# One layout [w, sample] for all activations, and group statistics by TensorE, in a four-layer residual net

## The chip, the cores and the metric

The kernel runs on one core of one Trainium2 chip. The metric is the time on the device in microseconds, the median of several runs. The core has five engines that run side by side and wait for each other through semaphores: TensorE (PE in the profile; its weight loads are shown as PEld), VectorE (DVE), ScalarE (ACT), GpSimd (POOL) and SyncE (SP), which here only issues DMAs. TensorE reads SBUF and writes PSUM[...].

## The reference

The input x has 8192 samples of 8 channels, 16 rows (h) and 16 columns (w). Four layers follow each other, and each adds the result of a layer to the unnormalized x. `_gn` normalizes over 4 groups of 2 channels.

```python
x = x + tt_matvec([core0, core1, core2], _gn(x)) + bias                # layer 0: three small factors, rank 8
x = x + relu(batchnorm(conv3x3(_gn(x), lin_w) + lin_b.sum(0)))         # layer 1: statistics over all samples
# layer 2: both sides quantized to 127 steps, one scale over all of _gn(x)
x = x + conv3x3(quantize(_gn(x)), quantize(weight)) / (sx * sw) + bias
# layer 3: weights are signs times a mean, padding repeats the edge
x = x + conv3x3(pad_edge(_gn(x)), sign(weight) * mean|weight|) + bias
```

## The kernel before, in words

**Tiles.** 128 samples make a tile, so there are 64 tiles of 128 partitions x 2048 floats. A partition is a pair (channel, row); along the free axis lie the 128 samples and the 16 columns w. Convolutions over rows and channels are matmuls with a banded 128 x 128 matrix, and the three taps over w are three matmuls whose moving operand is shifted by one column. Before, the free axis of x and all that comes of it is [sample, w]: the 16 columns of a sample lie side by side. The input is brought into that order on the host, as "xt"; a second copy, "xb", has another order that layer 0 contracts first.

**Stage 1 (lines 319 to 677)** does layer 0 and the convolution of layer 1. The loop runs over 256 quarter tiles n of 32 samples. `expand` contracts w into u (rank 8 x w) for the next quarter, in two groups k of 8 matmuls; each group fills the PSUM tile pu, of which there is one (`ps_u`, bufs=1), and `act.copy` moves it to u (2048 elements a partition). `main` multiplies u by core01 in eight accumulating matmuls r = 0 to 7 into po; a fp32 matmul shows as two instructions. The order is written out: `at(r, ...)` puts a step ahead of the r-th matmul of `main`. The first group of `expand` stands at r = 0, the second at r = 4. `norm_sums` and `norm_b_square` issue a square on ScalarE at r = 1 in two of four quarters, `limbs` a cast at r = 2; `conv1_scaled` follows at r = 6 and the two evacuations of `conv1` at the end. po, pm and pc share three PSUM slots (`ps_m`), so each po needs that the former po has been added to x by VectorE. `norm_sums` and `norm_stats` reduce x and its square over w (`reduce_w`), in the quarter q = 0 of the next tile. `conv1_output` writes y with w in steps of four.[...]

**Stage 2 (lines 745 to 857)** reads x and y from DRAM, applies batch norm and relu, adds, and takes the statistics of layer 2: `sums_pe` (8 matmuls of 512 columns into four strips of 32 PSUM partitions), a reduction over w and a transpose on VectorE (`stats2`), a power on GpSimd, and `to_rows` (a masked copy and a transpose on VectorE) with two matmuls in `spread2`. `centre2` subtracts the mean, `range2` takes the largest magnitude. Most tiles go back to DRAM; 13 stay in SBUF.

**Stage 3 (lines 879 to 1053)** does layers 2 and 3. For each tile: `scale2` (v, int8), `round2` (q, bf16), `layer2` (12 matmuls pq), `first2` on VectorE for one half and `second2` and `add2` on ScalarE and GpSimd for the other, the statistics of layer 3 (`square3`, `sums3`, `stats3`, `pow3`, `rows3`, `spread3`), `scale3` (t), `high3` and `low3` (t split in two fp32r parts, rows of 16 columns with an edge on each side, 18 in all), `layer3` (24 matmuls pf), `add3` and `finish`. The order of the steps of different tiles is C_HEAD, then TURN repeated, then C_TAIL (lines 48 to 69 and 1040 to 1047).

The access to u and the copy that fills it, and the one that fills core01 at the start:

```python
pu = ps_u.tile([P, 4, 2, 2 * R * W], F32, name=f"pu_{t}_{q}_{k}", tag="pu")
act.copy(T[t]["u", q][:, 16 * k:16 * k + 16].rearrange("p b n -> p (b n)"), pu.rearrange("p i j n -> p (i j n)"))
c01v = core01.rearrange("p s (n h) -> p n h s", n=C)
act.copy(c01v[:, n:n + C // 2], cps[:, n:n + C // 2].rearrange("p n (h s) -> p n h s", s=R))
```

Of the kernel before, what the change touches and what calls it, by code (L numbers as in the profile page):

```python
# [47 lines left out]
C_HEAD = """  # L48
rows2:0 spread2:0 v:0 rows2:1 q:0 spread2:1 c2h1:0 rows2:2 bias:0 v:1 spread2:2 rows2:3 c2h0:0 v:2 z1:0 q:1
spread2:3 stz:0 add1:0 bias:1 c2h1:1 sq:0 c2h0:1 z1:1 v:3 sums:0 stz:1 small:0 q:2 add1:1 c2h0:2 c2h1:2 bias:2  # L50
rows2:4 pow:0 sq:1 rows2:5 rows3:0 z1:2 spread2:4 spread3:0 stz:2 t:0 q:3 sums:1 hi:0 c:0 small:1 v:4 add1:2 pow:1
bias:3 c2h0:3 spread2:5 rows3:1 sq:2 c2h1:3 spread3:1 stz:3 lo:0 sums:2 t:1 rows2:6 corr:0 edl:0 small:2 c:1 q:4
z1:3 hi:1 c3h0:0 pow:2 c3h1:0 v:5 add1:3 rows3:2 out0:0 bias:4 out1:0 lo:1 sq:3 q:5 spread3:2 spread2:6 c2h0:4 c:2
corr:1 edl:1 c2h1:4 rows2:7 z1:4 stz:4 t:2 hi:2 sums:3 c3h1:1 small:3 v:6 c3h0:1 out1:1 c2h1:5 pow:3 bias:5 rows3:3
spread3:3 lo:2 out0:1 q:6 spread2:7 rows2:8 z1:5 edl:2 v:7 c:3 add1:4 sq:4 c2h0:5 c3h0:2 bias:6 t:3 corr:2 stz:5
sums:4 c3h1:2 small:4 add1:5 hi:3 out0:2 c2h0:6 pow:4 rows3:4 sq:5 out1:2 spread2:8 stz:6 spread3:4 t:4 lo:3 c2h1:6
z1:6 corr:3 edl:3 sums:5 c:4 hi:4 small:5 pow:5 bias:7 v:8 q:7 add1:6
""".split()
C_TAIL = """
c2h1:-4 sq:-5 rows2:-2 rows3:-6 out1:-8 spread3:-6 rows2:-1 spread2:-2 c2h0:-4 v:-2 sums:-5 stz:-4 z1:-4 q:-3 t:-6  # L60
edl:-7 c3h0:-7 q:-2 small:-5 c2h1:-3 c:-6 out0:-7 c2h0:-2 hi:-6 add1:-4 sq:-4 pow:-5 rows3:-5 z1:-3 spread3:-5
bias:-2 t:-5 stz:-2 lo:-6 edl:-6 sums:-4 small:-4 bias:-3 corr:-6 c:-5 spread2:-1 c2h0:-3 stz:-3 pow:-4 c3h1:-7
hi:-5 out1:-7 c3h0:-6 rows3:-4 spread3:-4 add1:-3 c2h1:-2 sq:-3 lo:-5 z1:-2 out0:-6 v:-1 c3h1:-6 edl:-5 q:-1 add1:-2
sums:-3 t:-4 corr:-5 c:-4 c3h1:-5 out1:-6 small:-3 sq:-2 pow:-3 hi:-4 out1:-5 lo:-4 rows3:-3 bias:-1 sums:-2 c2h1:-1
small:-2 z1:-1 spread3:-3 edl:-4 c2h0:-1 c3h0:-5 c:-3 t:-3 stz:-1 add1:-1 pow:-2 corr:-3 rows3:-2 c3h1:-4 hi:-3
spread3:-2 sq:-1 out0:-5 c:-2 corr:-4 sums:-1 t:-2 lo:-3 hi:-2 small:-1 pow:-1 out1:-4 c3h0:-4 corr:-2 rows3:-1
out0:-4 edl:-3 c3h0:-3 spread3:-1 t:-1 lo:-2 c3h1:-3 out0:-3 edl:-2 out1:-3 hi:-1 c:-1 lo:-1 c3h0:-2 c3h1:-2 edl:-1
out0:-2 c3h0:-1 out1:-2 corr:-1 c3h1:-1 out0:-1 out1:-1
""".split()

# [8 lines left out]
def tile_net(ctx: ExitStack, tc: tile.TileContext, xb, xt_in, pack0, pack1, pack2, out):  # L79
# [84 lines left out]
    def late_constants(late):  # L164
# [99 lines left out]
        mod32 = const.tile([P, 32], F32, name="mod32")  # L264
# [5 lines left out]
        for k, name in enumerate(("sel0", "sel1", "corr")):  # L270

            t = L[name] = const.tile([P, CH], F32, name=name)
            dve.tensor_copy(t.rearrange("p (g n) -> p g n", g=G),
                            mod32[:, G * k:G * k + G].unsqueeze(2).to_broadcast([P, G, CH // G]))
        yield "statistics"

    def diagonal(n):
        ts = []
        for k in range(2):
            t = const.tile([P, NQ, 32], F32, name=f"diag_{n}_{k}")  # L280
            nc.gpsimd.memset(t, 0.0)
            ts.append(t)
        return ts
# [6 lines left out]
    HALVES = [(0, P // 2), (P // 2, P)]  # L290

    def samples(t):
        return t.rearrange("p (b w) -> p b w", w=W)

    def over_w(stat, a, b):

        return stat[:, a:b].unsqueeze(2).to_broadcast([P, b - a, W])

    def reduce_w(dst, src, op=ALU.add):
        for a, b in HALVES:  # L300
            dve.tensor_reduce(dst[:, a:b], samples(src)[:, a:b], AX.X, op)
# [21 lines left out]
    with first as s:  # L323
# [13 lines left out]
        x1n = [const1.tile([P, P, W + 2], F32, name=f"x1n_{k}") for k in range(2)]  # L337
        for t in x1n:
            pool.memset(t[:, :, 0:W + 2:W + 1], 0.0)
# [13 lines left out]
        def add_bias(t):  # L353
            v = samples(T[t]["x"])
            pool.tensor_tensor(v, v, bias0_t.unsqueeze(1).to_broadcast([P, P, W]), ALU.add)
# [56 lines left out]
        def expand(t, q, k):  # L412

            if k == 0:
                T[t]["u", q] = us[q % 2].rearrange("p (b n) -> p b n", b=QS)
# [8 lines left out]
            else:  # L424
                xv = T[t]["xl", q].rearrange("p (i n m) -> p i n m", i=4, m=CH)
                for i in range(4):
                    for j in range(2):
                        pe.matmul(pu[:, i, j], xv[:, i, 2 * k + j], L["core2r"], start=True, stop=True)
            act.copy(T[t]["u", q][:, 16 * k:16 * k + 16].rearrange("p b n -> p (b n)"),
                           pu.rearrange("p i j n -> p (i j n)"))  # L430

        def main(t, q, between, n0=None):
            u = T[t].pop(("u", q)).rearrange("p b (s n) -> p b s n", s=R)
            po = ps_m.tile([P, BANK], F32, name=f"po_{t}_{q}", tag="mm")
            parts = [(0, QS)] if n0 is None else [(0, n0), (n0, QS)]
            for a, b in parts:
                for r in range(R):
                    for f, args in between.get(r, ()) if b == QS else ():
                        f(*args)
                    pe.matmul(samples(po)[:, a:b], core01[:, r], u[:, a:b, r, :], start=(r == 0), stop=(r == R - 1))  # L440
            cols = slice(q * BANK, (q + 1) * BANK)
            x = T[t]["x"]
            dve.tensor_tensor(x[:, cols], po, x[:, cols], ALU.add)
# [12 lines left out]
        def norm_apply(t):  # L456
            group_spread(spread1, T[t].pop("mv"), 32)
            x, xn = samples(T[t]["x"]), x1n[t % 2][:, :, 1:W + 1]
            for a, b in HALVES:
                for k, op, i in ((0, ALU.subtract, x), (1, ALU.mult, xn)):  # L460
                    dve.tensor_tensor(xn[:, a:b], i[:, a:b], over_w(spread1[:, k], a, b), op)


        def quarter_stats(t, q):
            cols, x = slice(q * BANK, (q + 1) * BANK), T[t]["x"]
            sums = small.tile([P, 2, QS], F32, name=f"sq_{t}_{q}", tag="sums")
            act.activation(xh[:, cols], x[:, cols], AF.Square)
            for k, src in enumerate((x, xh)):
                dve.tensor_reduce(sums[:, k], samples(src)[:, q * QS:(q + 1) * QS], AX.X, ALU.add)
# [3 lines left out]
        def quarter_apply(t, q):  # L473
            spread = spreads[q % 2]
            group_spread(spread, T[t].pop(("mv", q)), 32)
            b = slice(q * QS, (q + 1) * QS)
            x, xn = samples(T[t]["x"])[:, b], x1n[t % 2][:, b, 1:W + 1]
            for k, op, i in ((0, ALU.subtract, x), (1, ALU.mult, xn)):
                dve.tensor_tensor(xn, i, over_w(spread[:, k], 0, QS), op)
# [4 lines left out]
        def conv1_scaled(t, q):  # L484

            x = x1n[t % 2][:, q * QS:(q + 1) * QS]
            x4, x2 = (wk.tile([P, QS, n], F32, name=f"{k}_{t}_{q}", tag=k, bufs=1) for k, n in (("x4", W), ("x2", W // 2)))
            act.activation(x4, x[:, :, 0:W], AF.Copy, scale=4.0)
            act.activation(x2, x[:, :, 1:W:2], AF.Copy, scale=2.0)
            T[t]["x4", q] = x4, x2  # L490

        def conv1_input(t, q):
            x = x1n[t % 2][:, q * QS:(q + 1) * QS]
            x4, x2 = T[t].pop(("x4", q))
            e, r = (wk.tile([P, n, QS, W // 4], F32, name=f"{k}_{t}_{q}", tag=k, bufs=1) for k, n in (("e", 4), ("r", 2)))
            v = wk.tile([P, 6, QS, W // 4], F32, name=f"v_{t}_{q}", tag="v")
            pool.tensor_tensor(e.rearrange("p k b j -> p b j k"), *(t.rearrange("p b (j k) -> p b j k", k=4)
                                                                    for t in (x[:, :, 2:W + 2], x4)), ALU.subtract)
            pool.tensor_tensor(r[:, 0], x2[:, :, 1:W // 2:2], x2[:, :, 0:W // 2:2], ALU.subtract)
            pool.tensor_tensor(r[:, 1], x[:, :, 4:W + 1:4], x[:, :, 2:W:4], ALU.subtract)  # L500
            pool.tensor_tensor(v[:, 0], e[:, 2], e[:, 1], ALU.add)
            pool.tensor_tensor(v[:, 1], e[:, 2], e[:, 1], ALU.subtract)
            pool.tensor_tensor(v[:, 2], r[:, 1], r[:, 0], ALU.add)
            pool.tensor_tensor(v[:, 3], r[:, 1], r[:, 0], ALU.subtract)
            pool.tensor_tensor(v[:, 4:6], e[:, 2:4], e[:, 0:2], ALU.subtract)
            T[t]["v", q] = v.rearrange("p i b j -> p i (b j)")
# [14 lines left out]
        def conv1_direct(t, q):  # L521

            x = x1n[t % 2][:, q * QS:(q + 1) * QS]
            po = ps_m.tile([P, BANK], F32, name=f"pd_{t}_{q}", tag="mm")
            for k in range(3):
                pe.matmul(samples(po), L["band1"][:, k], x[:, :, k:k + W], start=(k == 0), stop=(k == 2))
            act.activation(T[t]["y"][:, q * BANK:(q + 1) * BANK], po, AF.Identity, bias=L["b1"], scale=1.0)
# [5 lines left out]
        def conv1_stats(t, q):  # L533
            dve.bn_stats(T[t]["bst"][:, q], T[t]["y"][:, q * BANK:(q + 1) * BANK])
# [6 lines left out]
        def conv1_output(t, q):  # L541
# [7 lines left out]
            s1, d3, d1, s3 = sd[:, 0], sd[:, 1], pm[:, 1], pm[:, 3]  # L549
            y = T[t]["y"][:, q * BANK:(q + 1) * BANK].rearrange("p (n k) -> p k n", k=4)  # L550
            ends = wk.tile([P, 2, NC], F32, name=f"ends_{t}_{q}", tag="ends", bufs=1)
            dve.tensor_tensor(ends[:, 0], s1, po[:, 0], ALU.add)
            dve.scalar_tensor_tensor(ends[:, 1], d3, 8.0, po[:, 1], ALU.mult, ALU.add)
# [154 lines left out]
    def sums_pe(ps, x, sq):  # L708

        for k, src in ((0, x), (1, sq)):  # L710
            for q in range(NQ):
                pe.matmul(ps[32 * q:32 * q + 32], L["wsum"][:, k], src[:, q * BANK:(q + 1) * BANK],
                          start=(k == 0), stop=(k == 1))


    def put_quarter(ps):
# [406 lines left out]
```

## Time and profile before

| | |
|---|---|
| median of 3 runs | 3833.41 us (3831.76 to 3834.64) |
| span of the profiled execution | 3831.5 us |
| PE, DVE, POOL, ACT busy | 94%, 89%, 79%, 66% |
| moved by DMA | 960.93 MB, mean 251 GB/s |

A row of the profile names engine, operation, output<-input by the program's names, the shapes, the count, then the busy time in all, the mean ns of one, and the idle time of the engine before it with what ended it. Busy time counts overlapping instructions once, so the mean of a matmul, which holds its latency, is longer than the distance from one to the next. The profiled execution is one run; its span is compared with what is worked out from its rows.

### The profile page before, as it was taken

The numbers are of one execution on the slowest core, as the hardware profiler recorded it, in microseconds if no ns is written. First come the engines' busy times: TensorE is split into PE (matmuls) and PEld (weight loads), VectorE is DVE, ScalarE is ACT, GpSimd is POOL, SyncE is SP. The second block draws the span as 40 slices with busy tenths as digits, with TensorE's granted clock in tenths as the row PEclk, the third lists the DMA queues.
The fourth block names the chain that finished last, engine by engine and source line by source line (L and its number), as shares of the span: only waits on it lengthen the run. The fifth ranks groups of instructions, "written<-read, shape, count | busy, mean of one in ns | idle before, by whom it ended". The sixth has DMA issues, their size and how long they took to land. (4 is left out here: it accounts for less than half of the span.)

```text
span 3831.5 us, 52833 instructions
## 1 busy us (share of the span) xinstructions
PE 3606.5 (94%) x16326; PEld 2127.6 (56%) x16326; DVE 3406.9 (89%) x6319; ACT 2513.1 (66%) x2673; POOL 3040.9 (79%) x3101
## 2 busy tenths in 40 slices
PE   8999999999999999999999999997655599999998
PEld 4666666666666666666666666662211155555555
DVE  8988888888888888888888888877998889999997
ACT  5666666666666666666666666665665477777775
POOL 4877778777777787777777877766887779999997
PEclk9999999999999999999999999998776699999999
DMA  5787787888877878788788788757999724444432
GB/s 212 255 268 258 258 266 251 270 253 262 270 256 258 267 250 271 253 262 267 258 261 266 250 271 252 258 187 281 422 425 425 301 110 176 187 185 178 185 145 99
DMA packets 210809, 960.93 MB, mean 251 GB/s; under 512 B 44896, under 2 KB 45152, under 8 KB 110048
## 3 DMA queue, kind: packets, MB, share of 16 engines
q1 hardware_dynamic: 173808, 692.22, 48.7%
q0 software_dynamic: 36288, 264.26, 23.4%
q8 instruction: 131, 2.15, 0.2%
q14 instruction: 150, 1.23, 0.1%
q10 hardware_dynamic: 432, 1.08, 0.1%
HBM read 578.84 MB, written 378.54 MB: 250 GB/s over the span
## 5 line engine op out<-in xcount | busy, mean ns | idle before, releaser
L43 PE MATMUL po<-u,core 128*128 128x512 f32 (+1 forms) x4112 | 1844.7, 591 | 0.0
L43 ACT COPY u<-pu 128x2048 f32<-128x2048 f32 x512 | 956.7, 1868 | 511.9 <-PE pu L43 511.8
L43 PEld LDWEIGHTS po<-u,core 128*128 128x128 f32 x4112 | 744.7, 190 | 737.1 <-issue 736.1
L43 PE MATMUL pu<-core2r,xl 128*128 128x256 f32 x4032 | 678.5, 310 | 4.5 <-ACT u L43 3.6
L43 PEld LDWEIGHTS pu<-core2r,xl 128*128 128x128 f32 x4032 | 527.9, 189 | 127.8 <-issue 123.0
L43 POOL TENSOR_TENSOR bs<-bs,xh 128x512 fp32r<-128x512 f32 (+1 forms) x253 | 325.6, 1287 | 201.0 <-ACT xh L43 200.9
L43 POOL TENSOR_TENSOR v<-e 128x128 f32<-128x128 f32 x750 | 397.9, 542 | 0.0
L43 DVE TENSOR_TENSOR xs<-po,xs 128x512 f32<-128x512 f32 x256 | 177.0, 692 | 217.5 <-PE po L43 217.5
L43 ACT ACTIVATE m<-pm,b 128x128 f32<-128x128 f32 x250 | 92.0, 368 | 395.5 <-PE pm L43 395.5
L43 PEld LDWEIGHTS pm<-v,fast 128*128 128x128 f32 x2000 | 262.5, 191 | 119.7 <-issue 106.2
L43 POOL TENSOR_TENSOR e<-x1n,x 128x512 f32<-128x512 f32 x250 | 306.2, 1225 | 23.9 <-ACT x L43 16.4
L43 DVE TENSOR_TENSOR bs<-bs,stat 128x1024 f32<-128x1024 f32 x252 | 290.8, 1217 | 2.1
L43 POOL TENSOR_TENSOR xs<-xs,w 128x2048 f32<-128x2048 f32 x64 | 291.5, 4554 | 0.6 <-DMA xs<-in_xt 0.6
L43 PE MATMUL pm<-v,fast 128*128 128x128 f32 x2000 | 263.6, 275 | 0.0
L43 ACT ACTIVATE x<-x1n 128x512 f32<-128x512 f32 x500 | 247.1, 545 | 7.6 <-DVE x1n L43 7.6
L43 POOL TENSOR_TENSOR mv<-mv,mhalf 128x4 f32<-128x4 f32 x127 | 130.8, 1030 | 138.1 <-DVE mv L43 138.1
L43 PE MATMUL pf<-hi,sign 128*128 128x512 f32 x768 | 227.7, 434 | 0.5 <-DVE xs L43 0.5
L43 POOL DMA_DIRECT2D xl<-limb_d x252 | 150.0, 595 | 96.9 <-ACT x L43 29.1
L43 PE MATMUL pf<-lo,sign 128*128 128x512 f32 x768 | 219.4, 423 | 0.0
L43 POOL TENSOR_TENSOR v<-r 128x128 f32<-128x128 f32 x500 | 215.9, 448 | 0.0
L43 ACT ACTIVATE sq<-xs 128x2048 f32<-128x2048 f32 x103 | 196.8, 1911 | 4.7 <-POOL xs L43 4.6
L43 PE MATMUL gb<-rows_c,sel 128*128 128x128 f32 x128 | 40.3, 409 | 167.3 <-DVE rows_c L43 167.3
(310 smaller groups left out, 7202.4 us busy)
## 6 DMA issues: line engine op xcount, KB each, us to landing
xl<-limb_d POOLq DMA_DIRECT2D x252, 1024.0 KB, 7.4
x_d<-xs SPq DMA_DIRECT2D x76, 1024.0 KB, 8.4
xs<-in_xt SPq DMA_DIRECT2D x64, 1024.0 KB, 7.5
bs<-in_xb SPq DMA_DIRECT2D x63, 1024.0 KB, 5.7
limb_d<-xh SPq DMA_DIRECT2D x1008, 64.0 KB, 4.3
limb_d<-bs SPq DMA_DIRECT2D x1008, 64.0 KB, 5.2
y_d<-ys SPq DMA_DIRECT2D x60, 1024.0 KB, 8.0
u<-x_d SPq DMA_DIRECT2D x34, 1024.0 KB, 5.9
```

The costliest lines, as they stand in the source:

```text
L43: return self.tc.keep_in_program_order(op(*args, **kwargs))
```

## The change

All activations of stage 1 to 3 become [w, sample]: for each column w the 128 samples lie side by side. Host code orders the input and the output so. In stage 1 ScalarE copies pu, which stays as it was, into u as [rank, w, sample]; reductions over w read with a step of 128 floats; y, x1n and v have whole runs of 32 samples. In stages 2 and 3 the reduction, transposes and masked copies of the statistics leave VectorE: `sums_pe` multiplies each w alone (32 matmuls of 128 columns, accumulating in one 128 x 128 PSUM tile), ScalarE copies the result, a matmul with eight columns folds it, and a spread is a ScalarE copy that repeats each of 4 values 32 times (`wide`) and one matmul with the identity. In stage 3 hi and lo are [w + 2, sample], so that a shifted operand is one run of 512; bias2 is no longer added to x but put into the square, the scaling and the last offset; both halves of layer 2 are added by VectorE, so that `bias2`, `second2` and `add2` go; the order of steps comes from sorting phases with a period instead of lists. The diff, cut:

```diff
+PERIOD = 10.78
+PHASE = {"wide": 0, "spread2": 0.01, "v": 0.02, "q": 11, "c2h0": 13.3, "stz0": 18.2, "c2h1": 19.6, "stz1": 21.4, "sq": 25.8,
...
     def reduce_w(dst, src, op=ALU.add):
         for a, b in HALVES:
-            dve.tensor_reduce(dst[:, a:b], samples(src)[:, a:b], AX.X, op)
+            dve.tensor_reduce(dst[:, a:b], by_w(src)[:, :, a:b].rearrange("p w n -> p n w"), AX.X, op)
...
         def add_bias(t):
-            v = samples(T[t]["x"])
-            pool.tensor_tensor(v, v, bias0_t.unsqueeze(1).to_broadcast([P, P, W]), ALU.add)
+            v = by_w(T[t]["x"])
+            pool.tensor_tensor(v, v, bias0_t.unsqueeze(2).to_broadcast([P, W, P]), ALU.add)
...
-                T[t]["u", q] = us[q % 2].rearrange("p (b n) -> p b n", b=QS)
+                T[t]["u", q] = us[q % 2].rearrange("p (n b) -> p n b", b=QS)
...
-            act.copy(T[t]["u", q][:, 16 * k:16 * k + 16].rearrange("p b n -> p (b n)"),
-                           pu.rearrange("p i j n -> p (i j n)"))
+            act.copy(T[t]["u", q][:, :, 16 * k:16 * k + 16].rearrange("p n b -> p b n"),
+                     pu.rearrange("p i j (b n) -> p (i j b) n", b=2))
...
-                    pe.matmul(samples(po)[:, a:b], core01[:, r], u[:, a:b, r, :], start=(r == 0), stop=(r == R - 1))
+                    pe.matmul(by_w(po)[:, :, a:b], core01[:, r], u[:, r, :, a:b], start=(r == 0), stop=(r == R - 1))
...
-            y = T[t]["y"][:, q * BANK:(q + 1) * BANK].rearrange("p (n k) -> p k n", k=4)
+            y = by_w(T[t]["y"])[:, :, quarter_of_samples(q)].rearrange("p (j k) b -> p k j b", k=4)
...
     def sums_pe(ps, x, sq):
         for k, src in ((0, x), (1, sq)):
-            for q in range(NQ):
-                pe.matmul(ps[32 * q:32 * q + 32], L["wsum"][:, k], src[:, q * BANK:(q + 1) * BANK],
-                          start=(k == 0), stop=(k == 1))
+            for w in range(W):
+                rows = slice(32 * (w % 4), 32 * (w % 4) + 32)
+                pe.matmul(ps[rows], L["wsum"][:, k], by_w(src)[:, w], start=(k == 0 and w < 4), stop=(k == 1 and w >= W - 4))
+    def fold_pe(st, rows):
+        pe.matmul(st, rows, L["mod32"][:, 0:2 * G], start=True, stop=True)
+    def wide(dst, src):
+        act.copy(dst.rearrange("p (g n) -> p g n", n=CH // G), src.unsqueeze(2).to_broadcast([P, src.shape[1], CH // G]))
+    def spread_pe(dst, col):
+        pe.matmul(dst, col, ident, start=True, stop=True)
-    def stats_small(mv, st, ps, name):
-        s = small.tile([P, 32], F32, name=f"s_{name}", tag="s")
-        dve.tensor_reduce(s, samples(ps), AX.X, ALU.add)
-        dve.transpose(st, s)
...
-    def to_rows(diag, mask, cols, name):
...
-        dve.transpose(rows, diag.rearrange("p q j -> p (q j)"))
-        return rows
...
             for a, b in HALVES:
-                dve.tensor_reduce(top[:, i % 4, a:b], samples(T[i]["x"])[:, a:b], AX.X, ALU.max,
+                dve.tensor_reduce(top[:, i % 4, a:b], by_w(T[i]["x"])[:, :, a:b].rearrange("p w n -> p n w"), AX.X, ALU.max,
                                   apply_absolute_value=True)
...
             on(i, sum2)
             on(i - 2, sums2)
+            on(i - 3, wide2)
+            on(i - 2, copy2)
             on(i - 3, spread2)
+            on(i - 2, fold2)
             on(i - 1, square2)
...
-        def second2(i):
-            act.activation(z3[i % 2], T[i].pop(("pq", 1)), AF.Identity, bias=L["bias2"], scale=inv)
-        def add2(i):
-            x = halves(T[i]["x"])[:, 1]
-            pool.tensor_tensor(x, x, z3[i % 2], ALU.add)
+        def first2(i, h):
+            x = halves(T[i]["x"])[:, h]
+            dve.scalar_tensor_tensor(x, T[i].pop(("pq", h)), inv, x, ALU.mult, ALU.add)
...
+        def turn3(i):
+            pe.matmul(turned, rows3[i % 2], ident, start=True, stop=True)
+        def rows_copy3(i):
+            T[i]["rows"] = small3.tile([P, P], F32, name=f"rows_{i}", tag="rows")
+            act.copy(T[i]["rows"], turned)
...
-            T[i]["hi"] = hi = wk.tile([P, P, W + 2], F32R, name=f"hi_{i}", tag="hi")
-            act.copy(hi[:, :, 1:W + 1], samples(T[i]["t"]))
+            T[i]["hi"] = hi = wk.tile([P, W + 2, P], F32R, name=f"hi_{i}", tag="hi")
+            act.copy(hi[:, 1:W + 1], by_w(T[i]["t"]))
...
-                        pe.matmul(samples(pc[:, k]), L["sign3"][:, n], tv[:, :, n:n + W],
+                        pe.matmul(pc[:, k], L["sign3"][:, n], T[i][t][:, 4 * q + n:4 * q + n + 4].rearrange("p w n -> p (w n)"),
                                   start=(m == n == 0), stop=(m == 1 and n == 2))
```

## The prediction

> **What bounds the kernel now.** I read the stage windows first, then the order in time of TensorE and ScalarE in stage 1, the chain of waits of stage 3, and last the rows of single shapes that price an access pattern. The windows (start and length, busy time of PE, PEld, DVE, ACT and POOL with counts, clock, DMA share, GB/s) show stage 1, stage 2 and stage 3:
>
> ```profile
> 0.00:2480.00 2480.00, 2461.86 (x10754) 1524.85 (x10755) 2202.27 (x4229) 1599.25 (x1810) 1892.52 (x2592) 1.00 0.80 259
> 2570.00:2980.00 410.00, 263.01 (x1255) 95.73 (x1253) 363.15 (x606) 239.32 (x243) 314.19 (x138) 0.75 0.91 379
> 3060.00:3832.00 772.00, 746.99 (x3712) 436.12 (x3712) 699.75 (x1233) 576.98 (x509) 710.95 (x254) 0.98 0.41 158
> ```
>
> Stage 1 is TensorE at full clock. Stage 2 is DMA: its windows stand at a share of 1.01 and 424 GB/s from 2680 to 3000 us. Stage 3 is TensorE again, with POOL and DVE close behind. One quarter tile of stage 1, PE and then ACT:
>
> ```profile
> 1205.41 3.60 PE L43 MATMUL po<-u,core 128*128 128x512 f32 x8
> 1208.44 1.50 PE L43 MATMUL pu<-core2r,xl 128*128 128x256 f32 x8
> 1209.78 3.60 PE L43 MATMUL po<-u,core 128*128 128x512 f32 x8
> 1213.21 1.05 PE L43 MATMUL pm<-v,fast 128*128 128x128 f32 x8
> 1214.10 0.61 PE L43 MATMUL pc<-v,fast 128*128 128x128 f32 x4
> 1214.47 1.18 PE L43 MATMUL pu<-core2r,xl 128*128 128x256 f32 x8
> 1215.48 3.60 PE L43 MATMUL po<-u,core 128*128 128x512 f32 x8
> ...
> 1205.61 1.87 ACT L43 COPY u<-pu 128x2048 f32<-128x2048 f32 x1 [0.87 <-PE pu L43]
> 1207.90 1.92 ACT L43 ACTIVATE sq<-bs 128x2048 f32<-128x2048 f32 x1 [0.42 <-DMA bs<-in_xb]
> 1209.72 0.60 ACT L43 CAST xh<-bs 128x512 fp32r<-128x512 f32 x1
> 1210.23 1.86 ACT L43 COPY u<-pu 128x2048 f32<-128x2048 f32 x1
> ```
>
> From po to po is 10.07 us: two halves of po at 3.43 (1209.78 to 1213.21), two groups of pu at 0.94 (4.37 between the po starts less 3.43), pm and pc 1.3. There is one pu tile in PSUM. So the second pu group can't start before ScalarE has copied the first, and 3.43 us of po is what covers that copy. A copy of 1.87 us fits; this is the cover that the change draws on.
>
> Stage 3, three pieces of the chain of waits (start, length):
>
> ```profile
> 3300.81 1.31 PE pq L43 x6
> 3304.09 1.85 PE s L43 x16
> 3305.94 6.42 PE pf L43 x24
> 3315.64 1.85 PE s L43 x16
> ```
>
> The period is 11.55 us, and PE alone fills it: s 1.85, pf 6.42, pq 2 x 1.31, three small products 0.66.
>
> The prices, ACT and DVE rows of the first microseconds:
>
> ```profile
> L43 ACT CAST xh<-bs 128x512 fp32r<-128x512 f32 x4 | 2.3, 622 | 0.0
> L43 ACT COPY core<-cps 128x512 f32<-128x512 f32 x2 | 1.9, 1039 | 3.3 <-PE cps L43 3.3
> ...
> L43 DVE TENSOR_REDUCE shz<-ident 128x16 f32<-128x128 f32 x1 | 0.4, 368 | 0.8 <-POOL ident masks.py:199 0.8
> L43 DVE TENSOR_REDUCE own<-ident 128x8 f32<-128x128 f32 x1 | 0.3, 277 | 0.0
> ```
>
> Both ACT rows write 512 elements; core writes each to a place 512 bytes from the last (line 584), xh side by side. Both DVE rows read 128; shz reads 64 bytes apart.
>
> **What the Trainium skill says.** "SBUF — State Buffer", Specifications: lines of 16 bytes, "need ≥2 hits per line for full bandwidth; each cross to a new line pays a penalty". The trace agrees: core pays (1039 - 622) / 512 = 0.81 ns an element over xh, shz (368 - 277) / 128 = 0.71. "TensorE: Matmul & The Clock Gate", Specs table: ScalarE's queue is strict first in, first out; the lines above show sq and xh between the two copies in program order. "TensorEngine Tiling (Array Packing)", Key Properties: different tiles can load and multiply in parallel; here 16 products of s take 1.85 us, or 0.116 each, where one po product takes 0.43.
>
> **The change, stage 1.** The po operand, xs, x1n, y and v keep their counts and sizes; add_bias now repeats a value along the inner axis (such an add, xs<-xs,c, takes 3.70 us in stage 3, the present form 4.56), on a POOL that has 24% idle. None of it shortens PE, whose po products already run at 0.43 us. What costs is the copy u<-pu: 2048 elements, each 128 bytes from the last. At the price of core it takes 1.87 + 2048 x 0.81 ns = 3.54 us. Bounds: 1.87 if 128 bytes were free, 4 us if worse than 512. I take 3.54.
>
> A walk through a quarter, t = 0 where the first pu group begins. po from 0.94; the copy starts 0.20 later (1205.41 to 1205.61) and ends at 4.68. po's half ends at 4.37. A pu group that waited starts 0.05 after the copy ends and costs 1.07 rather than 0.94 (copy 27.46 to 29.33, pu 29.38, po 30.45). So po resumes at 5.80 rather than 5.31: a loss of 0.49 us. The second copy starts at 5.94 and ends at 9.48, before PE gets to the next quarter at 10.54. In two of four quarters a square of 1.92 and the cast of 0.6 stand between the copies; then the second copy runs from 7.04 to 10.58, the next pu group waits until 10.63 and loses 0.22 with its slow start, and behind the copy stand x (1.0) and m (0.6), which delay the next first copy by some 0.15. Such a quarter loses about 0.85. A tile: 2 x 0.49 + 2 x 0.85 = 2.7 us.
>
> DVE: four reductions a tile (s<-xs, s<-sq, 1024 elements each) now read 512 bytes apart: at 0.71 ns each +0.73 us, 2.9 a tile; bounds 0.09 (a fixed start cost) and 1.07 (a whole cycle each; a row of 1024 takes 1.21). Back come four y writes a quarter, which leave their 16-byte steps: 0.41 to 0.28 (as ends<-sd,pc), 0.49 a quarter. All of the 2.9 falls in one quarter, where DVE now runs from 1193.86 to 1203.16 with 0.23 idle, before it adds po. po's PSUM slot is needed again 2.1 us after po ends. DVE needs 9.07 + 2.9 - 0.49 = 11.5 us there and is some 0.9 us late; as that delay also gives the next copy time, I keep 0.4. Stage 1: 3.1 us x 63 tiles less a little = +190 us.
>
> **Stage 2.** Off DVE go s_c 0.65, psc 0.23, diag_b 0.18 and rows_c 0.31 a tile (1.37); the two top reductions gain 1.46. ACT gains a spread copy of 256 and one of 128 (0.45 and 0.26 as x<-x1n and m<-pm), PE 64 small products for 16 at the same column count. All lies beside a full DMA queue whose bytes are unchanged. New waits: the spread copy stands behind the relu, which waits for y; centring a tile, and so its store, waits for it. Three tiles of slots cover that. I take +4 (-5 to +25; the upper end is two whole-cycle reductions a tile while DVE is 98% busy, 2680 to 2840).
>
> **Stage 3.** PE: pf reads 512 values in one piece instead of 32 runs of 16. A half pass of po takes 0.214 us, and pu's 256 columns 0.118, so a pf product costs between 0.214 and 0.235 instead of 0.267; 0.225 gives 5.4 for 6.42. Kept: pq 2.62, r2, r3, o3 0.66. New: turning the rows 0.22, the fold 0.22. The 64 products of s have the same columns in four strips: 1.85 if their weight loads overlap as now, up to 7 if each load took pm's 0.11 us alone; I take 2.0. Sum 11.1, against 11.55. DVE: v 2.34, stz 2.5, t 2.45, out 2.5, two small 0.3 = 10.1. POOL: lo and the correction 4.55 each (full rows, as xs<-xs,yk), pow 1.02 = 10.1. ACT loses bias and z1 (2.36) and gains 1.2 of small copies. So PE still ends last: 64 x 0.45 = 29 us. Head and tail are ordered by phases instead of lists; between 3065 and 3826 only about 23 us exceed 64 x 11.55, and I see no gain there. -30 (-55 to +10).
>
> **Sum.** 3831.5 (span of this execution) + 190 + 4 - 30 = 3995.5; the median of the runs is 1.9 above the span, so 3997, and I say 3995.
>
> **Rivals.** (a) The copy stays under its cover: stage 1 unchanged, 3833.4 + 4 - 30 = 3807, faster. Place: the wait of the second pu group for ScalarE. Price: nothing while a copy is shorter than 3.43 - 0.20 - 0.05 = 3.18 us, which is 0.64 ns an element over today. For it: at 0.81 the excess is small, and the second core copy starts only 0.82 us after the first. Against: what PE waits for is the end, and both ended after some 1.04 us. (b) The reductions decide: at a whole cycle an element the full quarter is late by 1.4 us more, 1.4 x 63 = 88 in stage 1, and 20 in stage 2: 4100. For: the y writes pay about that, 0.97 ns. Against: shz shows 0.71. (c) The 64 products are bound by their loads: +4 to 5 us a tile, some 300 us: 4270. Against: four loads of s start within 0.16 us now.
>
> **How the numbers follow.** Forecast 0.69 (3995, by itself 3925 to 4065), (a) 0.13, (b) 0.12, (c) 0.04, and 0.02 for a copy just at the edge, where stages 1 and 3 cancel. 0.2% is about what a measurement of this kernel can tell. Faster 0.13, same 0.02, slower 0.85. The range 3890 to 4110 holds the forecast, (b) and the milder copies, and leaves (a) and (c) out.
>
> **What would show it.** u<-pu near 3540 ns; PE idle before pu, released by ACT u, some 0.4 us in nearly every quarter; stage 1 at 10.7 to 10.8 us a quarter; s<-xs reductions near 1940 ns; pf pieces near 5.4 us in stage 3. A copy below 3.2 us, or a stage 1 that ends by 2570 us as now, proves the forecast wrong.

## The result, and the profile after

The changed kernel takes 4112.8 us (median of 4 runs, 4112.4 to 4113.1) against 3833.9 us before (4 runs, 3831.8 to 3834.6): a ratio of 1.0729, 95% interval 1.0714 to 1.0744. It is slower by 279 us. The forecast was 3995 us, range 3890 to 4110: the sign was right, the size was 118 us short, and the range was missed by 3 us.

The stages, cut at the same three places in both traces: the start of the first product mps_ of the batch statistics, the start of GpSimd's reduction over the partitions into gm (before: 3063.4 us, after: 3283.4 us), and the end of the last product of pf. What follows pf is 1.3 us longer than before.

| us | before | after | difference | forecast |
|---|---|---|---|---|
| stage 1, to mps_ | 2622.2 | 2835.8 | +213.6 | +190 |
| stage 2, to gm | 441.2 | 447.6 | +6.4 | +4 |
| stage 3, to the end of pf | 761.7 | 820.2 | +58.5 | -30 |

So three quarters of the loss is where the forecast put it, and a fifth is in a stage for which it had promised a gain.

The windows of the changed kernel, one in each stage (start and length, then busy time of PE, PEld, DVE, ACT and POOL with counts, clock, DMA share, GB/s):

```profile
0.00:2480.00 2480.00, 2349.28 (x9941) 1402.64 (x9942) 2142.78 (x3907) 2246.23 (x1670) 1714.24 (x2384) 1.00 0.74 239
2800.00:3210.00 410.00, 267.77 (x3952) 217.09 (x3950) 371.63 (x375) 264.04 (x344) 316.96 (x124) 0.72 0.94 389
3280.00:4050.00 770.00, 695.70 (x6662) 501.11 (x6726) 604.60 (x622) 458.24 (x671) 594.72 (x180) 0.99 0.39 149
```

In stage 1 ScalarE goes from 1599 to 2246 us busy in 2480, while TensorE falls from 2462 to 2349: it now waits. In stage 3 TensorE falls from 97% to 90% of the window, and no other engine is above 80%: so no new engine is at its limit, and a wait must be looked for.

A stretch of stage 1 after the change, TensorE first, then ScalarE (start, duration of the group, and in brackets the idle time before it and who ended it):

```profile
1205.24 0.61 PE L43 MATMUL pc<-v,fast 128*128 128x128 f32 x4
1205.61 1.18 PE L43 MATMUL pu<-core2r,xl 128*128 128x256 f32 x8
1206.62 3.60 PE L43 MATMUL po<-u,core 128*128 128x512 f32 x8
1210.67 1.20 PE L43 MATMUL pu<-core2r,xl 128*128 128x256 f32 x8 [0.45 <-ACT u L43]
1211.71 3.60 PE L43 MATMUL po<-u,core 128*128 128x512 f32 x8
...
1216.04 0.61 PE L43 MATMUL pc<-v,fast 128*128 128x128 f32 x4
1216.61 1.21 PE L43 MATMUL pu<-core2r,xl 128*128 128x256 f32 x8
1218.41 1.98 PE L43 MATMUL po<-u,core 128*128 128x512 f32 x4 [0.59 <-DVE xs L43]
...
1206.82 3.80 ACT L43 COPY u<-pu 128x2048 f32<-128x2048 f32 x1 [0.85 <-PE pu L43]
1210.43 1.90 ACT L43 ACTIVATE sq<-xs 128x2048 f32<-128x2048 f32 x1
1212.23 0.60 ACT L43 CAST xh<-bs 128x512 fp32r<-128x512 f32 x1
1212.74 3.82 ACT L43 COPY u<-pu 128x2048 f32<-128x2048 f32 x1
```

The copy begins 0.20 us after po, at 1206.82, and ends at 1210.62. po's products end at 1210.22, but the second group pu starts only at 1210.67, 0.05 us behind the copy. From po to po it is 5.09 us (1206.62 to 1211.71), where it was 4.37 before. The square and the cast hold up the next copy, which ends at 1216.56; the pu of the next quarter starts at 1216.61, again 0.05 us behind it, and 0.57 us after pc where it was 0.37 at 1205.24. At 1218.41 the other cost of the change is seen: po waits 0.59 us for DVE, which is late with the previous sum because of its reductions, and also because it stood idle for 0.75 us until the square, held up by the slow copy, was there. Three rows of the page, the last of them one of the two reductions (count, then busy us, mean ns, and the idle time before):

```profile
L43 ACT COPY u<-pu 128x2048 f32<-128x2048 f32 x512 | 1934.3, 3778 | 256.4 <-PE pu L43 255.7
...
L43 PEld LDWEIGHTS pu<-core2r,xl 128*128 128x128 f32 x4032 | 510.6, 188 | 287.3 <-ACT u L43 281.3
...
L43 DVE TENSOR_REDUCE s<-xs 128x64 f32<-128x1024 f32 x126 | 244.3, 1982 | 0.0
```

Stage 3, the chain of waits over one tile of 12.49 us (start, length; the time from the first pq 3599.90 to the same pq of the next tile, 3612.39):

```profile
3599.90 1.26 PE pq L43 x6
3601.16 1.89 PE ps_t L43 x64
3603.05 0.42 PE ps_a L43 x2
3603.47 1.42 PE pf L43 x6
...
3604.91 1.91 ACT hi L43
3606.82 0.27 ACT S_d L43
...
3607.22 0.46 PE ps_t L43 x2
...
3612.39 1.26 PE pq L43 x6
```

The chain leaves TensorE in the middle of pf. There, hi of an earlier tile has been read for the last time, which frees its buffer (there are two); ScalarE, which stood waiting for it, casts the next hi, and only then takes the next instruction of its queue, S_d, the copy of the sums. TensorE finishes the products of pf with lo in the meantime, and then stands for 0.94 us until S_d is done, before it may turn the rows (ps_t x2). So the wait goes round in a ring: TensorE waits for a copy that stands behind a cast that waits for TensorE. The waits of stage 3, 3500 to 4000 us (total, times, longest), name the two links:

```profile
ACT hi L43 <- PE pf L43: 140.4, 40, 3.5
...
PE ps_t L43 <- ACT S_d L43: 37.7, 40, 0.9
```

### The profile page after: what moved, and what is told of

Read it like the earlier page. It is cut to its first block, busy times and chain, and to the rows that moved or that the text cites. A ratio compares the mean times of both kernels' runs of the same rounds, so it can differ in the third digit from the quotient of the medians.

```text
span 4111.3 us, 65657 instructions
## 1 busy us (share of the span) xinstructions
PE 3700.1 (90%) x22793; PEld 2369.9 (58%) x22856; DVE 3481.3 (85%) x5481; ACT 3313.0 (81%) x2996; POOL 2946.4 (72%) x3036
## 5 line engine op out<-in xcount | busy, mean ns | idle before, releaser
L43 ACT COPY u<-pu 128x2048 f32<-128x2048 f32 x512 | 1934.3, 3778 | 256.4 <-PE pu L43 255.7
L43 PE MATMUL pu<-core2r,xl 128*128 128x256 f32 x4032 | 614.4, 294 | 86.8 <-ACT u L43 86.8
L43 PEld LDWEIGHTS pu<-core2r,xl 128*128 128x128 f32 x4032 | 510.6, 188 | 287.3 <-ACT u L43 281.3
L43 DVE TENSOR_REDUCE s<-sq 128x64 f32<-128x1024 f32 x126 | 243.3, 1973 | 46.9 <-ACT sq L43 46.9
L43 DVE TENSOR_REDUCE s<-xs 128x64 f32<-128x1024 f32 x126 | 244.3, 1982 | 0.0
L43 POOL TENSOR_TENSOR xs<-xs,w 128x2048 f32<-128x2048 f32 x64 | 230.6, 3603 | 0.7 <-DMA xs<-in_xt 0.6
L43 POOL TENSOR_TENSOR mv<-mv,mhalf 128x4 f32<-128x4 f32 x63 | 65.3, 1037 | 231.0 <-DVE mv L43 154.4
L43 PE MATMUL pf<-lo,sign 128*128 128x512 f32 x768 | 200.9, 397 | 2.3 <-POOL lo L43 2.3
L43 POOL TENSOR_TENSOR lo<-sq,hi 128x2048 fp32r<-128x2048 f32 x32 | 146.5, 4579 | 70.9 <-ACT hi L43 68.2
L43 POOL TENSOR_TENSOR lo<-xh,hi 128x2048 fp32r<-128x2048 f32 x32 | 146.5, 4578 | 69.1 <-ACT hi L43 69.1
```

Of the source, the lines that this page charges most:

```text
L43: return self.tc.keep_in_program_order(op(*args, **kwargs))
```

## The experiments

Theory T: stage 1 loses because the copy of u is longer than its cover, and next to that because DVE is late once a tile; stage 3 loses because of the ring hi, S_d, turning. The rivals: the reductions decide stage 1 (B), and in stage 3 TensorE's own work or another engine sets the period (E). All times stand beside runs of the kernel before on the same chip, whose medians are 3832.8 to 3833.9 us. The changed kernel, e7, e11, e13, e14 and e15 were run 4 to 17 times, the others once; the runs of one kernel lie within 4 us of each other (8 us in e13). The stages are read from one trace of each run.

| run | edit of the changed kernel | us | stage 1 ends | stage 3 lasts |
|---|---|---|---|---|
| after | none | 4112.8 | 2835.8 | 820.2 |
| e1_b_inner | copy of u, sample innermost | 3956.3 | 2677.5 | 820.4 |
| e2_copy_flat | copy of u side by side | 3957.6 | 2679.6 | 819.9 |
| e3_reduce_flat | reductions side by side | 4102.9 | 2826.0 | 819.8 |
| e6_inner_redflat | e1 and e3 | 3896.2 | 2617.1 | 820.3 |
| e4_S_early | S ahead of hi | 4041.1 | 2834.8 | 749.2 |
| e9_turn_apart | turned rows in ps_o | 4063.3 | 2834.7 | 771.2 |
| e10_run2 | copy of u in pairs | 3964.0 | 2686.0 | 820.3 |

**The copy.** In e1_b_inner the layout of u and the values stay; only the order in which ScalarE walks through them is another.

```diff
-            act.copy(T[t]["u", q][:, :, 16 * k:16 * k + 16].rearrange("p n b -> p b n"),
-                     pu.rearrange("p i j (b n) -> p (i j b) n", b=2))
+            act.copy(T[t]["u", q][:, :, 16 * k:16 * k + 16],
+                     pu.rearrange("p i j (b n) -> p n (i j b)", b=2))
```

> The changed kernel, but ScalarE walks u in the order in which it lies: sample innermost, so that it writes runs of 16 values side by side and reads PSUM 512 bytes apart. Theory T (the copy u<-pu, 3.78 us, is longer than the 3.43 us of po that cover it): the copy falls to 1.9 to 2.2 us, the wait of pu for ScalarE goes, the quarter tile of stage 1 falls from 10.90 to 10.1 to 10.3 us, stage 1 by some 150 to 190 us, and the whole to about 3940 us (3915 to 3985). Rival B (the strided reductions on DVE decide stage 1): the copy falls as well, but the quarter stays above 10.7 us and the whole above 4065 us. Rival P (a strided read of PSUM costs as much as a strided write of SBUF): the copy stays near 3.7 us and nothing changes, 4113 us.

For e2_copy_flat both sides of the copy run straight through, so that u no longer holds the order that the products need:

```diff
-            act.copy(T[t]["u", q][:, :, 16 * k:16 * k + 16].rearrange("p n b -> p b n"),
-                     pu.rearrange("p i j (b n) -> p (i j b) n", b=2))
+            act.copy(T[t]["u", q].rearrange("p n b -> p (n b)")[:, 16 * P * k:16 * P * k + 16 * P],
+                     pu.rearrange("p i j n -> p (i j n)"))
```

> The changed kernel, but the copy u<-pu writes side by side and reads side by side, as before the change, so the values of u stand in another order than the products of stage 1 need: this part of the computation is changed. Theory T: copy 1.87 us, quarter 10.1 to 10.3 us, the whole about 3940 us (3915 to 3985), as in the run with sample innermost or a few us below it. Rival B (reductions decide): above 4065 us.

The row of the copy on the page of e1_b_inner (busy us, mean ns, idle before it):

```profile
L43 ACT COPY u<-pu 128x2048 f32<-128x2048 f32 x512 | 955.3, 1866 | 565.9 <-PE pu L43 565.9
```

3778 ns became 1866, as long as before the change, and ScalarE now waits for pu instead of pu for ScalarE. Stage 1 is 158 us shorter. Rival B and rival P fall: a read of PSUM at steps of 512 bytes costs ScalarE nothing here (the copy of e2, which reads side by side, takes 1867 ns), while a write of SBUF at steps of 128 bytes doubled its time. e2 ends 1.3 us from e1.

**The reductions.** The edit of e3_reduce_flat reads other values, side by side:

```diff
-            dve.tensor_reduce(dst[:, a:b], by_w(src)[:, :, a:b].rearrange("p w n -> p n w"), AX.X, op)
+            dve.tensor_reduce(dst[:, a:b], src.rearrange("p (n w) -> p n w", w=W)[:, a:b], AX.X, op)
```

> The changed kernel, but the reductions over w (sums of the group norm of stage 1, maxima of stage 2) read 16 values side by side, so they add up other values than the group norm needs: this part of the computation is changed. The reductions fall from 1980 to about 1210 ns. Theory T (copy decides): the quarter tile falls only where DVE was late, from 10.90 to some 10.75 us, the whole to about 4075 us (4050 to 4105). Rival B: the quarter falls to 10.1 to 10.3 us, the whole to about 3950 us.

The reductions of stage 1 fell to 1215 ns as expected, and the stage gained 10 us. The maxima of stage 2, which the expectation names too, are written elsewhere and were not touched (1948 ns as in the changed kernel). The waits from 800 to 1600 us in e3 (total, times, longest) show what was left:

```profile
PEld pu L43 <- ACT u L43: 93.8, 75, 1.3
```

In the changed kernel the same stretch has 79.9 us of this wait, and waits of po for DVE besides; with DVE on time these are gone, but the copy takes most of the gain. With both edits together:

> The changed kernel with both: ScalarE's copy with sample innermost, and the reductions over w reading side by side, so that they add up other values than the group norm needs (this part of the computation is changed). What is left of stage 1 after the first edit is 55 us more than before the change (its end at 2677.5 against 2622.2 us). Theory T (DVE, late by some 0.8 us once a tile behind its 512-byte reductions, is all the rest): stage 1 ends at 2622 to 2630 us, the whole falls by some 50 us from 3956 to about 3907 us (3900 to 3915). Rival R (the rest is something else in stage 1, such as the new reading pattern of po's operand): the stage ends at 2660 us or later, as the reductions alone were worth 10 us beside the slow copy; the whole above 3940 us.

Stage 1 ends at 2617.1 us, 5 us earlier than before the change; T held, though the stage ended 5 us and the whole 4 us below its band. The two costs hide each other: reductions are worth 10 us beside the slow copy (2835.8 to 2826.0) and 60 beside the fast one (2677.5 to 2617.1); the copy is worth 158 with late reductions and 209 without. No single number is "the cost of the reductions".

**What a line costs.** e10_run2 writes pairs:

```diff
-            act.copy(T[t]["u", q][:, :, 16 * k:16 * k + 16].rearrange("p n b -> p b n"),
-                     pu.rearrange("p i j (b n) -> p (i j b) n", b=2))
+            act.copy(T[t]["u", q][:, :, 16 * k:16 * k + 16].rearrange("p n (s b) -> p s n b", b=2),
+                     pu.rearrange("p i j (b n) -> p (i j) n b", b=2))
```

> The changed kernel with ScalarE's copy in an order that writes pairs: two values side by side (8 bytes), then a step of 128 bytes. Theory L (the price is for a line of 16 bytes that is touched once only, as the page on SBUF says; two hits per line are enough): the copy falls to 1.9 us, the whole to about 3956 us, as with 16 values side by side. Rival C (the price is 0.93 ns for each change of place, whatever its size): half as many changes, copy 2.8 us, which is under its cover of 3.43 us, so the whole is 3956 to 3985 us and only the copy's time tells. Rival N (a pair doesn't help at all): 3.78 us, 4113 us.

```profile
L43 ACT COPY u<-pu 128x2048 f32<-128x2048 f32 x512 | 1013.5, 1979 | 544.3 <-PE pu L43 541.8
```

Theory L holds, and not rival C, which asked for 2.8 us: of the 1912 ns that single values pay, pairs pay 113. The Trainium skill says this of SBUF ("SBUF — State Buffer", Specifications: two hits to a line of 16 bytes are needed for full bandwidth), and the trace agrees: the second hit takes away 94% of the price.

**The ring of stage 3.** e4_S_early alters one number, which places S_d before hi in ScalarE's queue.

```diff
-         "sums": 31.9, "S": 33.2, "fold": 36.4,
+         "sums": 31.9, "S": 32.9, "fold": 36.4,
```

> The changed kernel with one number of the phase table altered: S at 32.9 instead of 33.2, which puts ScalarE's copy S_d of the sums ahead of the cast hi of the tile before. Theory T (the 0.94 us a tile for which TensorE waits for S_d in stage 3 is lost on the path that sets the end): the wait goes, the period falls from 12.49 to about 11.55 us, the whole by some 60 us to about 4053 us (4040 to 4070). Rival E (another wait takes its place: hi comes later by S_d's time, or TensorE waits for DVE or POOL instead): the period stays above 12.2 us, the whole above 4095 us.

The chain of waits in e4, one tile:

```profile
3604.32 1.26 PE pq L43 x6
3605.58 1.88 PE ps_t L43 x64
3607.47 0.42 PE ps_a L43 x2
3607.89 2.80 PE pf L43 x12
3610.69 0.22 PE ps_t L43 x2
...
3612.50 0.32 PE ps_r L43 x2
3612.82 2.81 PE pf L43 x12
3615.63 1.26 PE pq L43 x6
```

All of it is TensorE, and the period is 11.31 us (3604.32 to 3615.63). The run fell by 72 us rather than 60, because the wait costs more than its 0.94: turning took 0.46 us behind the wait and takes 0.22 without it.

Why does turning need S_d at all? It doesn't read it. e9_turn_apart moves the place that it writes out of the PSUM tile that S_d reads, and leaves every queue as it was:

```diff
-        r2, r3, o3, turned = (t[:, 0:P] for t in (ps_a, ps_r, ps_o, ps_t))
+        r2, r3, o3, turned = ps_a[:, 0:P], ps_r[:, 0:P], ps_o[:, 0:P], ps_o[:, P:2 * P]
```

> The changed kernel, but the turned rows of stage 3 lie in the PSUM tile ps_o (beside o3) instead of ps_t (beside the sums that S_d reads); the order on every engine stays. Theory T1 (TensorE's turning waits for S_d only because both touch the tile ps_t, a write after a read): the wait of ps_t for S_d goes, the period falls from 12.49 to 11.3 to 11.6 us, the whole to 4041 to 4060 us. Rival T2 (it waits for ScalarE for its own operand, the row of means that ScalarE writes, or the product behind it waits in its place): the period stays above 12.2 us, the whole above 4095 us.

```profile
3608.08 0.22 PE ps_o L43 x2
...
3609.80 0.28 ACT rows L43
...
3610.12 0.49 PE ps_r L43 x2
```

Turning (3608.08) follows pf at once. T1 holds: the wait was for the tile, not for a value, since turned and the sums lie at different columns of it. The tile fills one bank (`[P, BANK]` in the kernel), so the run doesn't tell whether columns of the tile or of the bank are what may not be touched. The gain is 49 us and not 72, because S_d and rows are still late on ScalarE, and r3 now waits some 0.3 us for rows; the period of 11.70 us and the whole are just outside what was expected.

**A version that beats both.** With e1 and e4 together DVE is still late in stage 1, so its sums had to become cheaper without changing what they add up. Five runs, all with both edits:

| run | further edit | us | stage 1 ends | stage 3 lasts |
|---|---|---|---|---|
| e7_tree | both sums as trees of additions | 3936.4 | 2729.9 | 749.2 |
| e11_tree_sq | tree for the squares only | 3868.5 | 2662.7 | 748.6 |
| e12_tree_late | both trees late in the quarter | 3874.0 | 2668.4 | 749.3 |
| e14_pairs | squares written in pairs | 3826.6 | 2619.4 | 748.9 |
| e15_spread_early | e14, spread2 behind r3 | 3826.0 | 2620.3 | 747.6 |

The tree adds whole halves, which lie side by side:

```diff
+    def tree_w(dst, src, tmp):
+        n = F // 2
+        while n > P:
+            dve.tensor_tensor(tmp[:, 0:n], src[:, 0:n], src[:, n:2 * n], ALU.add)
+            src, n = tmp, n // 2
+        dve.tensor_tensor(dst, src[:, 0:P], src[:, P:2 * P], ALU.add)
...
-            reduce_w(T[t]["s"][:, 0], T[t]["x"])
+            half = wk.tile([P, F // 2], F32, name=f"half_{t}", tag="half", bufs=1)
+            tree_w(T[t]["s"][:, 0], T[t]["x"], half)
...
-            reduce_w(T[t]["s"][:, 1], sqs[1])
+            tree_w(T[t]["s"][:, 1], sqs[1], sqs[1])
```

> The changed kernel with three edits: the copy with sample innermost, S ahead of hi in stage 3, and in stage 1 the sums over w as a tree of additions of whole halves (1024, 512, 256, 128 elements side by side) in place of reductions that read 512 bytes apart. Theory T: the tree takes 2.1 to 2.6 us where two reductions take 3.95; stage 1 is back at 2622 to 2632 us, stage 3 stays at 11.3 us a tile; the whole 3834 us (3822 to 3845), no slower than the kernel before by more than 0.3%. Rival R (the gains overlap, because a new wait appears in stage 1): 3870 us or more.

T missed by some 100 us (ratio 1.0271, interval 1.0253 to 1.0288). DVE in e7, from the timeline (start, duration):

```profile
1205.07 4.08 DVE L43 TENSOR_TENSOR half<-xs 128x1024 f32<-128x1024 f32 x1
```

An addition of 1024 elements takes 4.08 us. GpSimd worked through its own additions in the same time; the last of them, from the same view on POOL, ended at 1208.05, and 1.1 us later DVE was done:

```profile
1207.34 0.71 POOL L43 TENSOR_TENSOR v<-e 128x256 f32<-128x256 f32 x1
```

The Trainium skill ("SBUF — State Buffer", SBUF: two separate sides) describes a pair of ports which DVE and GpSimd share under an exclusive lock, and which a DVE instruction with two inputs in SBUF needs. The trace agrees, from both sides. In 50 of the 55 tiles traced between 100 and 2400 us DVE's addition takes 4.05 to 4.13 us: the page has the lock held for one instruction, but here DVE waits through the whole run of GpSimd's. In a few of the other tiles DVE got in between, and GpSimd paid: at 156.51 us its addition r<-x1n took 1.50 us for the usual 0.45, and DVE's 1.22. Two runs tested it. e11_tree_sq keeps only the last of the three edits:

```diff
-            reduce_w(T[t]["s"][:, 1], sqs[1])
+            tree_w(T[t]["s"][:, 1], sqs[1], sqs[1])
```

> The changed kernel with the copy with sample innermost, S ahead of hi, and the tree of additions for the sums of squares only; the sums of x stay a reduction that reads 512 bytes apart. Theory T (in the run with two trees the first addition half<-xs took 3979 ns where sq<-sq took 1232, because both its operands lie in SBUF and GpSimd was at work: DVE was blocked until GpSimd's run of additions ended; the tree of squares falls where GpSimd is idle): the tree takes 2.65 us where two reductions take 3.9; DVE gains 1.2 us a tile, more than the 0.8 us it is late; stage 1 ends at 2617 to 2635 us, the whole 3826 us (3818 to 3840). Rival K (an addition tree is slow by itself, or DVE stays late): stage 1 ends at 2660 us or later, 3868 us or more.

e12_tree_late moves the two lines of the tree over x from norm_sums to norm_stats, which is issued three products later:

```diff
         def norm_stats(t):
-            reduce_w(T[t]["s"][:, 1], sqs[1])
+            half = wk.tile([P, F // 2], F32, name=f"half_{t}", tag="half", bufs=1)
+            tree_w(T[t]["s"][:, 0], T[t]["x"], half)
+            tree_w(T[t]["s"][:, 1], sqs[1], sqs[1])
```

> As the run with two trees, but the tree over x moved from the first product of the quarter to the fourth, ahead of the tree over the squares. Theory T (GpSimd's run of additions blocked it): half<-xs falls from 3979 to below 2000 ns, stage 1 from 2729.9 to 2617 to 2650 us, the whole to 3826 to 3855 us. Rival K (the addition is slow by where its operands lie): it stays near 4 us, the whole near 3936 us.

In e12 the same addition, moved to where GpSimd is idle (none of its instructions overlaps it in 53 of 56 tiles between 100 and 2400 us), takes a third of the time; the squares' addition, which ran in 1232 ns in e7, now meets GpSimd's bs<-bs,xh and pays in turn (rows by shape, 800 to 1600 us; mean ns second after the bar):

```profile
L43 DVE TENSOR_TENSOR sq<-sq 128x1024 f32<-128x1024 f32 x20 | 44.8, 2240 | 0.0
L43 DVE TENSOR_TENSOR half<-xs 128x1024 f32<-128x1024 f32 x20 | 24.3, 1214 | 0.0
```

So the mechanism of T holds, and its sizes don't: e11 (1.0093, interval 1.0076 to 1.0110) came out at the numbers of its rival K, DVE still late, and e11 and e12 left stage 1 some 40 us too long, as their trees ran into GpSimd again (sq<-sq 1958 ns in e11 in this stretch). A reduction has one input and was never blocked: s<-xs stays between 1922 and 1992 ns in e11. e14_pairs keeps it, and makes its reads cheap by what e10 had shown; the layout of x itself stays:

```diff
-            act.activation(sqs[1], T[t]["x"], AF.Square)
+            act.activation(sqs[1].rearrange("p (j n e) -> p j e n", n=P, e=2), T[t]["x"].rearrange("p (j e n) -> p j e n", n=P, e=2), AF.Square)
...
-            reduce_w(T[t]["s"][:, 1], sqs[1])
+            for a, b in HALVES:
+                dve.tensor_reduce(T[t]["s"][:, 1, a:b], sqs[1].rearrange("p (j n e) -> p n j e", n=P, e=2)[:, a:b], AX.XY, ALU.add)
```

> The changed kernel with the copy with sample innermost and S ahead of hi; in stage 1 ScalarE writes the squares of x1 so that two neighbouring w of a sample lie side by side (steps of 8 bytes instead of 4), and DVE's reduction of them reads such pairs. The sums of x are unchanged. Theory L (two hits to a line of 16 bytes are enough, for ScalarE's writes and for DVE's reads): the square stays at 1.92 us, s<-sq falls from 1.95 to 1.2 to 1.3 us, and since a reduction has one operand GpSimd can't block it; DVE gains 1.4 us a tile, more than the 0.8 it was late; stage 1 ends at 2617 to 2640 us, the whole 3826 us (3820 to 3845). Rival N (DVE's price is for any step, as pairs 512 bytes apart are still 64 places): s<-sq stays at 1.9 us, stage 1 at 2677, the whole at 3885 us.

Rows by shape of e14, 800 to 1600 us:

```profile
L43 DVE TENSOR_REDUCE s<-xs 128x64 f32<-128x1024 f32 x40 | 76.7, 1957 | 0.0
...
L43 DVE TENSOR_REDUCE s<-sq 128x64 f32<-128x1024 f32 x39 | 45.4, 1205 | 0.0
L43 ACT ACTIVATE sq<-xs 128x2048 f32<-128x2048 f32 x20 | 42.2, 2109 | 0.0
```

In one trace, on one engine: single values 512 bytes apart 1957 ns, pairs 1024 bytes apart 1205. ScalarE pays 0.19 us for the square. e14 takes 3826.55 us (17 runs) against 3833.18 (29 runs), a ratio of 0.9983, interval 0.9976 to 0.9990: faster than both kernels, though by only 0.17% against the one before. Its gain over that is in stage 3 (761.7 to 748.9 us); stage 1 is 2.7 us shorter, and stage 2 6.8 us longer.

The last pair of runs asks for the 0.42 us of the small product spread2 (ps_a, between the sums and pf). A first try, made on e11 and not on e14, moved it behind r3:

```diff
-PHASE = {"wide": 0, "spread2": 0.01, "v": 0.02,
+PHASE = {"wide": -6.3, "spread2": -4.85, "v": 0.02,
...
-        r2, r3, o3, turned = (t[:, 0:P] for t in (ps_a, ps_r, ps_o, ps_t))
+        r2, r3, o3, turned = ps_r[:, P:2 * P], ps_r[:, 0:P], ps_o[:, 0:P], ps_t[:, 0:P]
```

> The run with the tree of squares only, and in stage 3 the small product spread2 (ident x wide, 0.42 us between the sums and pf) moved behind r3, into the PSUM tile of r3, with its operand wide written earlier. Theory T (of the 0.42 us only the 0.11 to 0.22 of the product itself is its own, the rest is the change of operand kinds before and after it): TensorE's period falls from 11.31 to 11.05 to 11.25 us, the whole is 4 to 16 us below the run with the tree of squares only, about 3815 us. Rival S (the changes cost the same wherever they stand, or DVE's v finds a new wait): the period stays at 11.3 us or rises, no gain.

It took 4121.6 us (ratio 1.0752, interval 1.0736 to 1.0768), stage 3 alone 1001.1 us where e11 has 748.6. Its chain:

```profile
3611.96 1.99 ACT sq L43
3613.95 0.29 ACT hi L43
...
3614.32 0.19 ACT wide_d L43
...
3614.56 0.79 PE ps_r L43 x2
```

The operand wide_d, a copy of 0.19 us, stood behind the square in ScalarE's queue, and all of TensorE behind it: the same fault as S_d behind hi, made anew. In e15_spread_early, made on e14, it stands ahead of S and hi (the cut shows what differs from e13):

```diff
-PHASE = {"wide": -6.3, "spread2": -4.85, "v": 0.02,
+PHASE = {"wide": -10.3, "spread2": -4.85, "v": 0.02,
```

> The run with pairs, and in stage 3 the small product spread2 moved behind r3 as in the earlier run, but its operand wide is now written ahead of S and hi on ScalarE instead of behind the square. Theory T (the loss of the earlier run was the wait of ps_r for wide_d alone, and most of the 0.42 us of spread2 is the change of operand kinds around it): the wait goes, the period is 11.05 to 11.25 us against 11.31, stage 3 is 4 to 16 us shorter, the whole about 3816 us. Rival S (the 0.42 us belongs to leaving the 32-column products for pf's, and comes back at pf): period 11.3 us, no gain. Rival W (another wait, as S_d or hi behind wide): period above 11.5 us.

```profile
3601.45 0.55 PE ps_r L43 x4
...
3606.07 1.88 PE ps_t L43 x64
3607.95 2.99 PE pf L43 x12
```

Rival S holds: spread2 costs 0.23 us in its new place (0.55 less the 0.32 of r3 alone), and pf behind the sums now takes 2.99 us instead of 2.80. Of the 0.42 us, 0.19 falls on whatever product follows those of 32 columns, and stays. The period is 11.30 us as before; 3825.98 us (ratio 0.9981, interval 0.9973 to 0.9989) is e14 over again.

## Why the prediction was right and wrong

- **Stage 1, the copy.** Right in mechanism: the second group of pu waits for ScalarE. From po to po the quarter shown loses 0.72 us (5.09 for 4.37), where the walk had 0.49. The copy is 3.78 us, not 3.54: 0.93 ns an element over the 1.87 us, where the row of core gave 0.81. With DVE out of the way the copy is worth 209 us (e6 against e3), 3.3 us a tile; the sum had 2.7, or 170 us. This term was mis-sized.
- **Stage 1, the reductions.** 1.94 us forecast, 1.98 measured; "DVE late 0.9, kept 0.4" was 25 us for the stage. Measured beside the slow copy: 10 us; beside the fast one it is 60, or 0.96 a tile. y writes 0.28 us as forecast. The stage as a whole is +214 for +190: the copy 39 us above its term, the reductions 15 below, so the errors cancel in part, and that is luck.
- **Stage 2.** +6 for +4. The middle of the stage is at a DMA share of 1.01 and 424 GB/s after the change as before; which of the new work makes the 6 us was not tried.
- **Stage 3, the step that failed.** "So PE still ends last: 64 x 0.45 = 29 us" added up TensorE's products and took for granted that nothing new stands between them. The small copies on ScalarE were counted as busy time (1.2 us, on an engine with room), not as places in a queue. Nothing was asked of S_d: behind what it stands (hi, which waits for TensorE itself), and who waits for it (turning, through a shared PSUM tile). That is 0.94 us of waiting and 0.24 of a slow start a tile; e4 took away 71 us of stage 3 and e9 49. Without the wait the kernel (e4, 4041.1 us) lies inside the stated range.
- **Stage 3, the sizes.** TensorE's own work is 11.31 us, not 11.1: pf 5.61 for 5.4 (0.234 us a product, the upper bound of the text rather than the 0.225 chosen; the lower bound, half of a po product, was read from no row), small products 1.30 for 1.10 (the 0.19 of e15), against pq 2.50 for 2.62 and s 1.88 for 2.0. A gain was there, 0.24 us a tile: with the wait removed stage 3 is 12.5 us shorter than before the change. The wait and the sizes together are 64 x (12.49 - 11.1) = 89 us, which is the distance from -30 to +58.5.
- **The rivals.** (a), a copy that stays under its cover, is refuted by its duration. (c) too: 64 products take 1.88 us. (b) gave 4100 us, near what was measured, but for the wrong reason: with cheap reductions and the slow copy the kernel still takes 4103. A time that fits doesn't show a mechanism.
- **The range.** It ended at +10 for stage 3. The text listed no new wait there, so its upper end held none.

Not tried: the kernel of before with the new stage 3 alone, and this copy with single values at steps other than 128 bytes.

## What to carry to other kernels

When a change puts small copies on an engine with time to spare, don't add up its busy time: write down for each new copy what stands ahead of it in the queue, what that waits for, and who waits for the copy, through shared PSUM tiles too. Before choosing a layout, look at who writes it and reads it one value at a time; often only the order of the walk or a pairing of neighbours has to change, and not the layout. And take costs out one by one and together: two that hide each other look small alone.

## What the runs showed of the hardware

- ScalarE writing single fp32 values 128 bytes apart: 3778 ns for 2048, against 1866 in runs of 16 and 1979 in pairs. Reading PSUM 512 bytes apart in the same copy cost nothing.
- DVE reducing 1024 fp32 values: 1957 ns with single values 512 bytes apart, 1205 with pairs 1024 bytes apart.
- A DVE addition with both operands in SBUF stood for some 3 us until GpSimd's run of additions ended (4.08 us for 1.21); the same instruction moved to where GpSimd is idle took 1.21. Where DVE got in first, an addition of GpSimd took 1.50 us for 0.45. Reductions of DVE, with one input, kept their time beside GpSimd.
- 64 fp32 products of 32 columns in four strips took 1.88 us; the next product of the whole array then took 0.19 us longer, for both of the products that were put there.
- A product of TensorE into one part of a PSUM tile waited 0.94 us for a ScalarE copy that read another part of it; in another tile it did not wait.
